# A four-layer graph network: half of a gather and two sets of transposes placed behind their product, and small f32 matmuls turned into rounded ones with two-part operands

## The chip, the core and the metric

The kernel runs on one core of one Trainium2 chip. The metric is the device time of one execution in microseconds (us). An execution that was profiled has a span, from its first to its last instruction, and its own device time, which is a little more.

The engines have short names in the rows: PE is the matmul engine (TensorE), PEld its weight loads, DVE is VectorE, ACT is ScalarE, POOL is GpSimd, and SP (SyncE) issues most of the DMAs.

## The reference

Four layers work on x, of shape 8 x 2048 x 64 (batch, nodes, features), with one 2048 x 2048 adjacency whose rows are normalised. Each layer is followed by a residual sum and a layer norm. Only what the change touches is shown.

```python
# layer 0: graph convolution with Chebyshev terms and weights made from node embeddings
As = [eye(N), A, 2 * A @ A - eye(N)]
x_g = einsum('knm,bmc->bnkc', stack(As), x)
out = einsum('bnki,nkio->bno', x_g, einsum('nd,dkio->nkio', embedding, weight)) + embedding @ bias

# layer 1: 64 hyperedges; H says which nodes belong to which edge
h = x @ W
s = leaky_relu(h @ a_node, 0.2)
alpha = softmax(where(H.T > 0, s, NEG))            # over an edge's nodes
agg = einsum('ben,bnf->bef', alpha, h)
beta = sigmoid((h @ a_gn)[:, None, :] + (agg @ a_ge)[:, :, None])
all_he = elu(beta * h + (1 - beta) * agg)          # per node and edge
coefs1 = softmax(where(H > 0, se, NEG))            # over a node's edges
g = einsum('bne,benf->bnf', coefs1, all_he)
```

Layers 2 and 3 are further products with the adjacency.

## The kernel before, in words

**Tiles and two-part operands.** The nodes are 16 tiles of 128. A tile of x is 128 rows of 512 columns (8 batches of 64 features). The adjacency is used as a 0/1 mask times a scale for each row. An operand of a large product is kept as two rounded parts, a high and a low one (`x_hi` and `x_lo`, `y_hi` and `y_lo`), that are multiplied by the mask one after the other. `r_(...)` marks an operand as rounded f32; such a matmul is one instruction on PE, and one whose operands are not marked is two.

**Order.** Inside `program_order()` the instructions of PE, DVE, ACT and POOL keep the order in which the code issues them. SP isn't bound in this way: its order is chosen by the planner that places the DMAs. Where a queue waits, all that stands behind it on that engine waits too.

**The first product** (`first_product`, matmuls at L569) makes y = A x for all tiles. It goes through 32 pieces of the adjacency, in four quarters of 8, with 512 target columns a quarter. A piece has two row tiles, and after the 8 matmuls of each row tile the loop may resume a generator of other work, `memberships`: once after the first row tile and twice after the second, from piece 9 on, and once in piece 6. At the end of each quarter ACT and DVE turn the sums into `y_hi` (L583) and `y_lo` (L584).

**The lists** (`memberships`) say for layer 1 which edges a node belongs to. Every `yield` ends a step. For each of four quarters q of the nodes: DVE makes `pT` (L382); PE counts with a triangular matrix into `pf` (L386); DVE makes `pfm` from it (L391, the tile is named `pT_raw`) and the first one-hot lists (L393, L396), whose stores and the next quarter's loads are issued there. Then come, for each of four tiles: `sm` on PE (L406) and `S` on DVE (L409, L412); `rk` on DVE (L419); a second matmul into `sm` (L424); its comparison on DVE (L429). `pf` and all `sm` share one PSUM buffer (tag `li`), so the next of them waits until DVE has read the one before.

**The end of the first product** transposes tile 0 of y (L594) for layer 0, then makes tile 0 of the second product, y2 = 2 A y (L603, scaled by ACT at L608).

**Layer 0** goes through the tiles j in order, each in eight groups of weight matmuls (`weigh`, PE L1446, DVE L1457). After the fifth group `visit(j)` does, on PE: the gather of tile j-2 into the edges' sums (L1651, a high and a low part), the first transposes of tile j+1 (`first_terms`), the second product of tile j+1 (`product`, L1403, 32 matmuls), in `counted` the degree (L1426) and the share of tile j-2 in the softmax denominators (L1430), the features' transposes `trx` of tile j-1, and the transposes `try2` of y2 of tile j+1 (`second_term`). ACT scales y2 (L1409) and then copies the denominators (L1432) and the degree (L1434). `weighted` makes what a later gather reads: the members' matrix `md`, and exp(score) times h in two parts (POOL L1638 and L1644, ACT L1643). PSUM buffers of tag `tr` are two, in turn.

**Layer 1** is performed by a list of tokens. For each tile, `sx` reads the terms of a node's at most three separate edges (L864), those of the shared slots (L868: `S` against `hgr`), and a transpose of `S`; `gates` on DVE (L884 to L889) forms gates and coefficients from them. `reciprocals` fills half of `hgr` (L808 to L810).

Lines are those of the kernel before.

Of the kernel before, what the change touches and what calls it, by code (L numbers as in the profile page):

```python
# [63 lines left out]
def kernel(  # L64
# [252 lines left out]
    def memberships(pre, ps, pm, fcw_sb, fcb_sb, fcg_sb):  # L317
# [60 lines left out]
        for q in range(NQ):  # L378
# [7 lines left out]
            nc.tensor.matmul(  # L386
                pf, r_(tri.rearrange("p h e -> p (h e)")), r_(pT), start=True, stop=True
            )
            yield
            pfm = raw  # L390
            nc.vector.tensor_tensor(pfm, pf, pT, ALU.mult)  # L391
            oh01 = pre.tile([P, QW], F32, tag="oh01", name=f"oh01_{q}", bufs=2)
# [60 lines left out]
    def first_product(own, pre, rawp, mskp, y_hi, y_lo, prepare, after, bias_in, midway, own_masks):  # L453

        x_hi, x_lo = buffer(own, 0, "x_hi"), buffer(own, 1, "x_lo")
        with tc.tile_pool(name="acc0", bufs=7, space=PSUM) as ps_acc, tc.tile_pool(
# [87 lines left out]
            with program_order():  # L544
# [43 lines left out]
                for _ in steps:  # L588
                    pass
                nc.vector.tensor_scalar(cols_of["s2"], cols_of["s1"], 2.0, None, op0=ALU.mult)  # L590
                tr = ps_acc.tile([P, NP, P], F32, tag="acc", name="try1_0")
                for pr in range(NP):
                    for part in (y_hi, y_lo):
# [6 lines left out]
                acc = ps_acc.tile([P, BC], F32, tag="acc", name="y2p_0")  # L600
                for mt in range(NT):
                    for part in (y_hi, y_lo):
                        nc.tensor.matmul(  # L603
                            acc, r_(own_masks[mt // 8][:, mt % 8, :]), r_(part[:, mt, :]),
                            start=mt == 0 and part is y_hi, stop=mt == NT - 1 and part is y_lo,
                        )
                y2 = own.tile([P, BC], F32, tag="b0_10", name="y2_0")
                nc.scalar.activation(y2, acc, AF.Copy, scale=cols_of["s2"][:, 0:1])  # L608
        return {"y1": y1T, "y2n": y2}

    @with_exitstack
    def layer1(
# [18 lines left out]
        mhalf = l1.tile([P, B], F32, tag="mhalf", name="mhalf")  # L631
        nc.gpsimd.memset(mhalf, -0.5)
        ext = l1.tile([P, 2, B], F32, tag="ext", name="ext")
        av32 = l1.tile([P, 32], F32, tag="av32", name="av32")
        nc.gpsimd.tensor_copy(av32, av_sb.to_broadcast([P, 32]))

# [70 lines left out]
        with tc.tile_pool(name="fa", bufs=2) as fa:  # L707
# [10 lines left out]
            with program_order():  # L718
# [135 lines left out]
        def units(j, dst):  # L854
# [4 lines left out]
            def sx():  # L859
                oh = l1.tile([P, 4, P], F32, tag="oh", name=f"oh_{j}", bufs=4)  # L860
                nc.sync.dma_start(oh, lists["oh"][j // 4][:, j % 4])
                sm = ps_s.tile([P, QW], F32, tag="sm", name=f"sx_{j}")
                for u in range(4):
                    nc.tensor.matmul(  # L864
                        sm[:, P + 16 * u:P + 16 * u + 16], r_(oh[:, u, :]), r_(extv),
                        start=True, stop=True,
                    )
                nc.tensor.matmul(  # L868
                    sm[:, P + 64:P + 80], S[:, j, :], hgr[:, j].rearrange("p k b -> p (k b)"),
                    start=True, stop=True,  # L870
                )
                transpose(sm[:, 0:P], S[:, j, :])
                t.update(oh=oh, sm=sm)
# [5 lines left out]
            def gates():  # L879
                gate = small("gate", f"gate_{j}", (P, 4, B))  # L880
                coef = small("coef", f"coef_{j}", (P, 4, B), 3)
                ex = t["sm"][:, P:P + 80].rearrange("p (u k b) -> p u k b", u=5, k=2)
# [385 lines left out]
    def layer0(  # L1268
# [6 lines left out]
        h_sb, wb, vecs, av_sb, pm, es, hgr, aggp, rden, early = layer1s  # L1275
        (raws, msk), terms, resid, norm, srow = begun, {}, {}, {}, {}
        x1s, xTs, hss, mds, scs, isplit, mms, tr15, dens = {}, {}, {}, {}, {}, {}, {}, [], {}

        homes = {"xT": (0, 1, 2), "xs": (3,), "ihi": (4,), "hs": (5,), "hsf": (15,), "y1T": (6, 7), "r": (8, 9),
                 "y2": (10,), "y2T": (11, 12), "cs": (13, 14)}  # L1280
# [141 lines left out]
        def counted(j, i):  # L1422

            dp = ps_tr.tile([P, QW], F32, tag="tr", name=f"dgp_{j}")
            if j < NT:
                nc.tensor.matmul(  # L1426
                    dp[:, 0:2], r_(msk[j, "sum"]), r_(ones_r), start=True, stop=True
                )
            if i >= 0:
                nc.tensor.matmul(dp[:, 8:8 + B], mds[i], es[:, i, :], start=True, stop=True)  # L1430
                dens[i] = tile("den", f"den_{i}", (P, B), 1)
                nc.scalar.copy(dens[i], dp[:, 8:8 + B])  # L1432
            if j < NT:
                nc.scalar.copy(deg[:, j:j + 1], dp[:, 0:1])  # L1434

# [193 lines left out]
        def weighted(j):  # L1629

            md = tile("md", f"md_{j}", (P, 2, E))
            nc.gpsimd.tensor_copy(r_(md), pm[:, j, :].unsqueeze(1).to_broadcast([P, 2, E]))
            mds[j] = md.rearrange("p h e -> p (h e)")
            if j < len(kept_i):
                for t, kept_part in zip(parts_of(j), kept_i[j]):
                    nc.sync.dma_start(kept_part, t)
            hs = tile("hsf", f"hs_{j}")
            nc.gpsimd.tensor_tensor(  # L1638
                b_view(hs), b_view(h_sb[:, j, :]), bcast(es[:, j, :]), ALU.mult
            )  # L1640
            hi = tile("hs", f"hs_hi_{j}")
            lo = tile("y1" if j == NT - 2 else "x1", f"hs_lo_{j}", bufs=1)
            nc.scalar.copy(r_(hi), hs)  # L1643
            nc.gpsimd.tensor_tensor(r_(lo), hs, hi, ALU.subtract)  # L1644
            hss[j] = hi, lo

        def gather(j):
            for part in hss[j]:
                if j == NT - 2 and part is hss[j][1]:
                    early[0](2)  # L1650
                nc.tensor.matmul(  # L1651
                    aggp, r_(mds[j]), r_(part), start=j == 0 and part is hss[0][0], stop=False
                )

        def spread():

# [43 lines left out]
        load_x(1)  # L1700
        def visit(j):

            when(j - 2, gather)
            if j < NT - 1:
                when(j - 1, normed, 1)
            when(j + 1, compare, 0)
            if j < NT - 1:
                when(j - 1, normed, 2)
            when(j + 1, first_terms)
            if j + 1 < NT:  # L1710
                for _ in product(j + 1):
                    pass
# [1 line left out]
            when(j + 2, mask, 1)  # L1714
            when(j + 1, compare, 1)
            counted(j + 1, j - 2)
            when(j - 1, to_features)
            if j == NT - 2:
                for t in range(len(kept_i)):
# [1 line left out]
                        nc.sync.dma_start(y[:, t, :], kept_part)  # L1721
            when(j + 1, second_term)
            if j == 2:
                nc.vector.tensor_copy(rden, dens[j - 2])
            elif j > 2:
                nc.vector.tensor_tensor(rden, rden, dens[j - 2], ALU.add)

        def last_tile():

            last = NT - 1  # L1730
            early[0](6)
            half_features(0)
            gather(last - 1)
# [969 lines left out]
```

## Time and profile before

| what | value |
|---|---|
| median of 3 runs | 1202.68 us (1201.78 to 1206.43) |
| the profiled execution | 1202.65 us |
| its span | 1200.9 us, 19838 instructions |
| granted TensorE clock | 0.998 |
| PE busy | 1179.7 us (98%) |
| DVE, POOL, ACT busy | 887.0 us (74%), 499.7 us (42%), 389.3 us (32%) |
| first product, 9 to 137 us | PE 125.32 busy of 128.00 |
| layer 0's visits, 171 to 620 us | PE 445.61 busy of 449.00, DVE 368.25 |
| layer 1, 664 to 936 us | PE 270.69 busy of 272.00, DVE 230.34 |

A row of the timeline gives the start and the duration in us, the engine, the line, the operation, what it writes and reads, and how many instructions were merged into it; in square brackets is how long the engine was idle before it and whom it waited for. The ends of matmuls are modelled and they overlap, so the distance between two starts says what a matmul costs. A row of the waits gives the waiting engine and line, whom it waited for, the total in us, how often, and the longest.

### The profile page before, as it was taken

The numbers are of one execution on the slowest core, as the hardware profiler recorded it, in microseconds if no ns is written. First come the engines' busy times: TensorE is split into PE (matmuls) and PEld (weight loads), VectorE is DVE, ScalarE is ACT, GpSimd is POOL, SyncE is SP. The second block draws the span as 40 slices with busy tenths as digits, with TensorE's granted clock in tenths as the row PEclk, the third lists the DMA queues.
The fourth block names the chain that finished last, engine by engine and source line by source line (L and its number), as shares of the span: only waits on it lengthen the run. The fifth ranks groups of instructions, "written<-read, shape, count | busy, mean of one in ns | idle before, by whom it ended". The sixth has DMA issues, their size and how long they took to land.

```text
span 1200.9 us, 19838 instructions
## 1 busy us (share of the span) xinstructions
PE 1179.7 (98%) x7502; PEld 942.4 (78%) x7502; DVE 887.0 (74%) x1677; ACT 389.3 (32%) x1005; POOL 499.7 (42%) x429
## 2 busy tenths in 40 slices
PE   9999999999999999999999999999999999999997
PEld 7877788888888888888887666666667888888886
DVE  4555668888888888888877788988887666665455
ACT  3100101222222222222223467767777321211111
POOL 2000392555545555555531489888871211100000
PEclk9999999999999999999999999999999999999999
DMA  8977852323332233333283313323220433434552
GB/s 287 250 226 226 180 166 94 113 91 117 117 112 94 94 108 117 117 117 115 80 298 137 111 71 114 99 77 106 97 71 1 148 133 106 140 106 168 183 175 73
DMA packets 101991, 157.10 MB, mean 131 GB/s; under 512 B 13056, under 2 KB 64640, under 8 KB 96256
## 3 DMA queue, kind: packets, MB, share of 16 engines
q1 hardware_dynamic: 97088, 151.51, 39.1%
q10 hardware_dynamic: 4368, 4.20, 1.0%
q8 instruction: 61, 1.00, 0.4%
q0 software_dynamic: 432, 0.05, 0.1%
q14 instruction: 42, 0.34, 0.1%
HBM read 117.97 MB, written 37.76 MB: 130 GB/s over the span
## 4 chain that ended last, share of the span: by engine, by line
PE 93%; DVE 2%; ACT 2%; DMA 1%; issue 1%; POOL 0%; SPq 0%; ACTq 0%; POOLq 0%; DVEq 0%
PE pp L1446 27%; PE a L1910 19%; PE ind L1910 10%; PE y2p L1403 9%; PE y1p L569 9%; PE fc L1028 3%; PE try L168 1%; PE yp L2009 1%; PE gp L929 1%; PE trm L168 1%; PE red L978 1%; PE u L1139 1%; PE hp L1571 1%; PE dp L947 1%; ACT y L1409 1%; PE aggp L1651 1%
## 5 line engine op out<-in xcount | busy, mean ns | idle before, releaser
L1457 DVE SCALAR_TENSOR_TENSOR r<-pp,emb_sb,r 128x256 f32<-128x256 f32 x512 | 247.6, 484 | 76.0 <-PE pp L1446 61.9
L1446 PE MATMUL pp<-w_sb,xT 64*128 64x256 f32 x1024 | 155.4, 380 | 0.6 <-DVE r L1457 0.6
L1446 PE MATMUL pp<-w_sb,y2T 64*128 64x256 f32 x1024 | 153.4, 376 | 0.0
L1446 PE MATMUL pp<-w_sb,y1T 64*128 64x256 f32 x1024 | 153.3, 376 | 0.0
L1315 POOL TENSOR_TENSOR ms<-msk,srow 128x1024 f32<-128x1024 f32 x30 | 76.2, 2540 | 89.9 <-DVE msk L449 89.9
L1446 PEld LDWEIGHTS pp<-w_sb,y2T 64*128 64x128 f32 x1024 | 99.3, 187 | 11.4 <-DVE y2T L1419 0.3
L1446 PEld LDWEIGHTS pp<-w_sb,y1T 64*128 64x128 f32 x1024 | 99.4, 187 | 11.2
L1446 PEld LDWEIGHTS pp<-w_sb,xT 64*128 64x128 f32 x1024 | 95.1, 187 | 12.9 <-issue 2.7
L569 PE MATMUL y1p<-x_hi,m 128*128 128x512 f32 x256 | 102.9, 402 | 0.7 <-ACT x_hi L471 0.7
L569 PE MATMUL y1p<-x_lo,m 128*128 128x512 f32 x256 | 100.5, 393 | 0.2 <-DVE x_lo L472 0.2
L1910 PE MATMUL a<-y_lo,mj_l 128*128 128x512 f32 x240 | 95.1, 396 | 0.0
L1910 PE MATMUL a<-y_hi,mj_l 128*128 128x512 f32 x240 | 95.0, 396 | 0.0
L1403 PE MATMUL y2p<-y_hi,msk 128*128 128x512 f32 x240 | 94.7, 395 | 0.0
L1910 PE MATMUL a<-v_hi,mj_l 128*128 128x512 f32 x240 | 93.9, 392 | 0.0
L1910 PE MATMUL a<-v_lo,mj_l 128*128 128x512 f32 x240 | 93.7, 391 | 0.0
L1403 PE MATMUL y2p<-y_lo,msk 128*128 128x512 f32 x240 | 93.6, 390 | 0.0
L1910 PE MATMUL ind<-y_hi,mj_l 128*128 128x512 f32 x208 | 90.5, 435 | 0.0
L1910 PE MATMUL ind<-y_lo,mj_l 128*128 128x512 f32 x208 | 81.8, 393 | 0.0
L964 POOL TENSOR_TENSOR ez<-ez,coef 128x1024 f32<-128x1024 f32 x32 | 61.6, 1926 | 11.1 <-DVE ez L959 11.0
L1355 DVE SCALAR_TENSOR_TENSOR ms<-ms,adj 128x1024 f32<-128x1024 f32 x30 | 66.2, 2206 | 0.0
L1638 POOL TENSOR_TENSOR hs<-h,es 128x512 f32<-128x512 f32 x15 | 15.7, 1043 | 115.8 <-ACT hgr L1610 115.8
L1111 POOL TENSOR_TENSOR r<-r,bias_sb 128x512 f32<-128x512 f32 x14 | 17.9, 1276 | 105.3 <-DVE r L2030 105.3
(347 smaller groups left out, 2460.5 us busy)
## 6 DMA issues: line engine op xcount, KB each, us to landing
mj_l<-mask SPq DMA_DIRECT2D x44, 1024.0 KB, 4.9
adj<-in_at SPq DMA_DIRECT2D x64, 256.0 KB, 3.8
mask<-msk SPq DMA_DIRECT2D x32, 512.0 KB, 4.5
raw<-in_at SPq DMA_DIRECT2D x31, 512.0 KB, 5.3
oh<-oh SPq DMA_DIRECT2D x32, 128.0 KB, 3.7
xT<-in_xt SPq DMA_DIRECT2D x16, 256.0 KB, 3.2
xs<-in_xn SPq DMA_DIRECT2D x16, 256.0 KB, 2.7
kept<-x SPq DMA_DIRECT2D x16, 256.0 KB, 3.6
```

The lines of the kernel that those rows point to most:

```text
L168: nc.tensor.matmul(dst, src, ident, start=True, stop=True, is_transpose=True)
L569: nc.tensor.matmul(accs[q][jj], r_(m[:, t, jj * P:(jj + 1) * P]), r_(part[:, mt, :]), start=i + h + t == 0 and part is x_hi, stop=i == 3 a ...
L964: nc.gpsimd.tensor_tensor(by_b(ezs[i]), by_b(ezs[i]), per_b(t["coef"], 2 * i, 2), ALU.mult)
L1028: nc.tensor.matmul(fcs[i][:, h, :], fcw_sb[rs], t["sT", i][rs], start=True, stop=True)
L1111: nc.gpsimd.tensor_tensor(b_view(t), b_view(t), bias2_sb.unsqueeze(1).to_broadcast([P, B, C]), ALU.add)
L1315: nc.gpsimd.tensor_tensor(ms, m, srow[j].unsqueeze(1).to_broadcast([P, 8, P]), ALU.mult)
L1355: nc.vector.scalar_tensor_tensor(ms, ms, 1.0, raws[j][h], op0=ALU.mult, op1=ALU.not_equal, accum_out=bad[:, 2 * j + h:2 * j + h + 1],)
L1403: nc.tensor.matmul(acc, r_(msk[j, mt // 8][:, mt % 8, :]), r_(part[:, mt, :]), start=mt == 0 and part is y_hi, stop=mt == NT - 1 and part ...
L1446: nc.tensor.matmul(pp[:, h, pl, :], terms[j][name][rs, 2 * bq + pl], w_sb[rs, k, dq * 4 * C:(dq + 1) * 4 * C], start=k == 0, stop=k == K - 1,)
L1457: nc.vector.scalar_tensor_tensor(rb, ppv[:, :, dd, :], emb_sb[:, j, d:d + 1], rb, op0=ALU.mult, op1=ALU.add)
L1638: nc.gpsimd.tensor_tensor(b_view(hs), b_view(h_sb[:, j, :]), bcast(es[:, j, :]), ALU.mult)
L1910: nc.tensor.matmul(acc, r_(a[:, mt, :]), r_(part[:, mt, :]), start=mt == 0 and part is hi, stop=mt == NT - 1 and part is lo,)
```

## The change

- In the first product, the transposes of tile 0 of y come behind the second product of tile 0 and ACT's scaling of it, instead of ahead of them.
- In a visit of layer 0, only the low part of the gather stands ahead of the product; in visits 2 to 14 the high part stands behind `counted`. In visit 0 the first transposes of tile 1 stand behind `counted` too.
- The denominators of tiles 0 to 13 are made from exp(score) in two rounded parts (`es2`, made by ACT and POOL in `weighted`), with one matmul of 16 columns; the 16 sums are added up in `dsum` and folded to 8 in the last visit.
- In layer 1, `hgr` is split into two rounded parts (`hgs`, two DVE operations in `reciprocals`, which runs twice), and the slots' terms are one rounded matmul of 32 columns, whose halves `gates` adds.
- In `memberships`, the `yield` between `pf` and `pfm` is gone.

```diff
@@ memberships
                 pf, r_(tri.rearrange("p h e -> p (h e)")), r_(pT), start=True, stop=True
             )
-            yield
             pfm = raw
             nc.vector.tensor_tensor(pfm, pf, pT, ALU.mult)
@@ first_product
                 nc.vector.tensor_scalar(cols_of["s2"], cols_of["s1"], 2.0, None, op0=ALU.mult)
+                (the product y2p_0 of 32 matmuls, and y2_0 = acc * s2 on ACT)
                 tr = ps_acc.tile([P, NP, P], F32, tag="acc", name="try1_0")
...
                 nc.scalar.copy(y1T, tr)
-                (the same product and y2_0)
@@ layer1
+        hgs = l1.tile([P, NT, 2, 2, B], F32, tag="hgs", name="hgs")
...
                     nc.vector.reciprocal(hgr[:, lo:hi, 1, :], rec)
+                    nc.vector.tensor_copy(r_(hgs[:, lo:hi, 0]), hgr[:, lo:hi])
+                    nc.vector.tensor_tensor(
+                        r_(hgs[:, lo:hi, 1]), hgr[:, lo:hi], hgs[:, lo:hi, 0], ALU.subtract
+                    )
...
-                    sm[:, P + 64:P + 80], S[:, j, :], hgr[:, j].rearrange("p k b -> p (k b)"),
+                    sm[:, P + 64:P + 96], r_(S[:, j, :]),
+                    r_(hgs[:, j].rearrange("p i k b -> p (i k b)")),
...
+                slot = small("slot", f"slot_{j}", (P, 2, B))
+                nc.vector.tensor_copy(slot, ex[:, 4])
+                nc.vector.tensor_tensor(slot, slot, ex[:, 5], ALU.add)
...
-                    nc.vector.tensor_copy(dst_[:, 3, :], ex[:, 4, k, :])
-                    nc.vector.tensor_tensor(dst_[:, 3, :], ex[:, 3, k, :], dst_[:, 3, :], op)
+                    nc.vector.tensor_tensor(dst_[:, 3, :], ex[:, 3, k, :], slot[:, k, :], op)
@@ layer0, counted
-                nc.tensor.matmul(dp[:, 8:8 + B], mds[i], es[:, i, :], start=True, stop=True)
-                dens[i] = tile("den", f"den_{i}", (P, B), 1)
-                nc.scalar.copy(dens[i], dp[:, 8:8 + B])
+                nc.tensor.matmul(
+                    dp[:, 8:8 + 2 * B], r_(mds[i]), r_(es2s[i].rearrange("p k b -> p (k b)")),
+                    start=True, stop=True,
+                )
+                dens[i] = tile("den", f"den_{i}", (P, 2 * B), 1)
+                nc.scalar.copy(dens[i], dp[:, 8:8 + 2 * B])
@@ layer0, weighted
+            if j < NT - 2:
+                es2s[j] = tile("es2", f"es2_{j}", (P, 2, B))
+                nc.scalar.copy(r_(es2s[j][:, 0, :]), es[:, j, :])
+                nc.gpsimd.tensor_tensor(
+                    r_(es2s[j][:, 1, :]), es[:, j, :], es2s[j][:, 0, :], ALU.subtract
+                )
@@ layer0, gather and visit
-        def gather(j):
-            for part in hss[j]:
-                if j == NT - 2 and part is hss[j][1]:
-                    early[0](2)
-                nc.tensor.matmul(
-                    aggp, r_(mds[j]), r_(part), start=j == 0 and part is hss[0][0], stop=False
-                )
+        def gather(j, i):
+            nc.tensor.matmul(
+                aggp, r_(mds[j]), r_(hss[j][i]), start=j == 0 and i == 1, stop=False
+            )
...
-            when(j - 2, gather)
+            for i in (1, 0) if j == NT - 1 else (1,):
+                when(j - 2, gather, i)
...
-            when(j + 1, first_terms)
+            if j:
+                when(j + 1, first_terms)
...
             counted(j + 1, j - 2)
+            if j == 0:
+                first_terms(1)
+            if 2 <= j < NT - 1:
+                gather(j - 2, 0)
             when(j - 1, to_features)
...
             if j == 2:
-                nc.vector.tensor_copy(rden, dens[j - 2])
+                sums.append(tile("dsum", "dsum", (P, 2 * B), 1))
+                nc.vector.tensor_copy(sums[0], dens[0])
             elif j > 2:
-                nc.vector.tensor_tensor(rden, rden, dens[j - 2], ALU.add)
+                nc.vector.tensor_tensor(sums[0], sums[0], dens[j - 2], ALU.add)
+            if j == NT - 1:
+                nc.vector.tensor_tensor(rden, sums[0][:, 0:B], sums[0][:, B:2 * B], ALU.add)
```

In the last tile the two parts of its gather are issued as before, with the same two steps of other work between them.

More of the change, by code (lines that the diff above doesn't have):

```diff
@@ L590, in first_product @@
                 nc.vector.tensor_scalar(cols_of["s2"], cols_of["s1"], 2.0, None, op0=ALU.mult)
+                acc = ps_acc.tile([P, BC], F32, tag="acc", name="y2p_0")
+                for mt in range(NT):
+                    for part in (y_hi, y_lo):
+                        nc.tensor.matmul(
+                            acc, r_(own_masks[mt // 8][:, mt % 8, :]), r_(part[:, mt, :]),
+                            start=mt == 0 and part is y_hi, stop=mt == NT - 1 and part is y_lo,
+                        )
+                y2 = own.tile([P, BC], F32, tag="b0_10", name="y2_0")
+                nc.scalar.activation(y2, acc, AF.Copy, scale=cols_of["s2"][:, 0:1])
                 tr = ps_acc.tile([P, NP, P], F32, tag="acc", name="try1_0")
@@ L599, in first_product @@
                 nc.scalar.copy(y1T, tr)
-                acc = ps_acc.tile([P, BC], F32, tag="acc", name="y2p_0")
-                for mt in range(NT):
-                    for part in (y_hi, y_lo):
-                        nc.tensor.matmul(
-                            acc, r_(own_masks[mt // 8][:, mt % 8, :]), r_(part[:, mt, :]),
-                            start=mt == 0 and part is y_hi, stop=mt == NT - 1 and part is y_lo,
-                        )
-                y2 = own.tile([P, BC], F32, tag="b0_10", name="y2_0")
-                nc.scalar.activation(y2, acc, AF.Copy, scale=cols_of["s2"][:, 0:1])
         return {"y1": y1T, "y2n": y2}
@@ L881, in gates @@
                 coef = small("coef", f"coef_{j}", (P, 4, B), 3)
-                ex = t["sm"][:, P:P + 80].rearrange("p (u k b) -> p u k b", u=5, k=2)
+                ex = t["sm"][:, P:P + 96].rearrange("p (u k b) -> p u k b", u=6, k=2)
+                slot = small("slot", f"slot_{j}", (P, 2, B))
+                nc.vector.tensor_copy(slot, ex[:, 4])
+                nc.vector.tensor_tensor(slot, slot, ex[:, 5], ALU.add)
                 for dst_, k, op in ((gate, 0, ALU.add), (coef, 1, ALU.mult)):
@@ L1277, in layer0 @@
         x1s, xTs, hss, mds, scs, isplit, mms, tr15, dens = {}, {}, {}, {}, {}, {}, {}, [], {}
+        es2s, sums = {}, []
         homes = {"xT": (0, 1, 2), "xs": (3,), "ihi": (4,), "hs": (5,), "hsf": (15,), "y1T": (6, 7), "r": (8, 9),
@@ L1645, in weighted @@
             hss[j] = hi, lo
-        def gather(j):
-            for part in hss[j]:
-                if j == NT - 2 and part is hss[j][1]:
-                    early[0](2)
-                nc.tensor.matmul(
-                    aggp, r_(mds[j]), r_(part), start=j == 0 and part is hss[0][0], stop=False
-                )
+        def gather(j, i):
+            nc.tensor.matmul(
+                aggp, r_(mds[j]), r_(hss[j][i]), start=j == 0 and i == 1, stop=False
+            )
         def spread():
@@ L1732, in last_tile @@
             half_features(0)
-            gather(last - 1)
+            gather(last - 1, 0)
+            early[0](2)
+            gather(last - 1, 1)
             denp = ps_p.tile([P, 2, 2, 4 * C], F32, tag="pp", name="denp")[:, 0, 0, 0:B]
```

## The prediction

> **What bounds the kernel now.** I read the page's first part and its chain first, then who TensorE (PE) waits for, then the timeline at the places that the diff touches.
>
> ```profile
> PE 1179.7 (98%) x7502; PEld 942.4 (78%) x7502; DVE 887.0 (74%) x1677; ACT 389.3 (32%) x1005; POOL 499.7 (42%) x429
> PE 93%; DVE 2%; ACT 2%; DMA 1%; issue 1%; POOL 0%; SPq 0%; ACTq 0%; POOLq 0%; DVEq 0%
> ```
>
> PE is busy for 98% of the span and makes 93% of the chain: what lengthens or shortens PE's own sequence counts in full, anything else only where PE waits for it. These are all of PE's waits that the diff can touch:
>
> ```profile
> PE try L168 <- ACT deg L1434: 4.2, 15, 0.8
> PE sm L406 <- DVE oh L429: 1.2, 3, 0.4
> PE sm L406 <- DVE pT_raw L391: 1.1, 1, 1.1
> PE try L168 <- ACT y L608: 0.8, 1, 0.8
> PE sm L424 <- DVE rk L419: 0.4, 1, 0.4
> ```
>
> The first and fourth follow a product in layer 0, and the diff moves matmuls into them. The other three lie in the first product, where the list steps are dealt out between its matmuls, and the diff takes one `yield` from these steps. A gap as it stands on PE (first product, third quarter):
>
> ```profile
> 98.98 0.40 PE L569 MATMUL y1p<-x_lo,m 128*128 128x512 f32 x1
> 99.22 0.22 PE L424 MATMUL sm<-S,rk 128*128 128x128 f32 x1
> 99.83 0.30 PE L406 MATMUL sm<-tri,pT 128*128 128x64 f32 x1 [0.39 <-DVE oh L429]
> 99.96 0.48 PE L569 MATMUL y1p<-x_hi,m 128*128 128x512 f32 x1
> 100.28 0.39 PE L569 MATMUL y1p<-x_lo,m 128*128 128x512 f32 x1
> ```
>
> Starts count here, since durations overlap; plain matmuls start 0.23 us apart. L424 and the next tile's L406 stand next to each other, and between them VectorE (DVE) must read the one PSUM buffer of tag `li` (L429). A visit of layer 0:
>
> ```profile
> 358.23 0.39 PE L1403 MATMUL y2p<-y_lo,msk 128*128 128x512 f32 x1
> 358.46 0.17 PE L1426 MATMUL dgp<-ones_r,both 128*128 128x2 f32 x1
> 358.48 0.37 PE L1430 MATMUL dgp<-es,md 128*128 128x8 f32 x2
> 358.71 0.64 PE L168 MATMUL trx<-ident,x 128*128 128x128 f32 x4
> 359.57 0.66 PE L168 MATMUL try<-ident,y 128*128 128x128 f32 x4 [0.23 <-ACT deg L1434]
> ```
>
> After the product, ScalarE (ACT) copies y2, den and deg (358.72 to 359.52), and only then may `try2` start, 1.34 us after the product's last matmul, however little PE has in between.
>
> **The change part by part.** *The removed `yield`.* The steps are resumed once after the first row tile of a piece and twice in a row after the second, from piece 9 on; eight product matmuls lie between the resumptions except inside the pair. Call resumption number c, c=0 being the lone one in piece 6: c mod 3 = 1 is the single one, 2 and 0 are the pair. Four segments precede quarter 0, and a quarter has 16 (pT, pf, pfm with the one-hots, then for each of four tiles sm, rk, L424 with the next segment beginning with L429). So `pf` falls on 2, 0, 1, 2 in the four quarters. The trace shows this: the L406 after pf comes 8, 16, 8, 8 product matmuls later, and only the third quarter has L424 and L406 as neighbours. Without the `yield` a quarter has 15 segments, a multiple of three: all four have `pf` on 2 and their first L406 on 0. Then every quarter has the third's order, and pf and the first L406 become neighbours too.
>
> Price of a neighbour pair L424/L406: from 98.98 to 100.28 are 1.30; two plain intervals are 0.46, and the two steps set apart cost 0.11 and 0.12 (58.65 to 59.22, 60.61 to 61.19). Lost: 0.61. Price of pf/L406: pf to DVE's L391 is 0.43 (93.34 to 93.77), L391 lasts 0.69, L406 starts 0.04 later (75.66 to 75.70): 1.16, with 0.23 ahead and 0.13 and 0.32 behind 1.84, less 0.46 and less 0.36 that they cost apart (0.24 and 0.12): 1.02. Queued behind the waiting L391 on DVE are the one-hots, S and the next piece's mask. The masks are about 9 us ahead (piece 16's done at 62.3, needed at 70.8), so PE doesn't run out of them. The step also issues four one-hot stores and two loads of the next quarter's lists on SP, whose queue then stands until DVE has the one-hots; behind them are the pieces' loads. The same lead covers that; uncovered, it is the kind of wait that DVE's masks had for loads (L527, 6.0 us in 5 waits), and I leave it at nothing.
>
> Before, by the same subtraction: second quarter 1.37 (74.20 to 76.15, L391 behind y_lo), third 0.61+0.61+1.26 (the last with y_lo ahead of rk), fourth 0.24: 4.1 us. After: 4 x 1.02 = 4.1, 12 x 0.61 = 7.3, again 0.65 where y_lo falls in the third quarter, and 1.4 in the second, where y_lo now stands between the first L406 and its L424 (DVE needs 1.4 for one-hots and S, 2.7 for y_lo, 0.7 for a mask, 0.5 for rk = 5.3, against 16 matmuls and L406's own, 3.9). Sum 13.5. **Net +9.4**; from +7 (if y_lo is covered) to +12 (if DVE is late at a third of the pairs by what y_lo cost).
>
> *Tile 0's transposes behind its product* (L594): eight at 0.11, 136.93 to 137.77 = 0.84, go into the gap 144.90 to 146.11 while ACT makes y2. But the third y2T matmul group already waits 0.30 for DVE's y2T (147.67), which is behind compares and a mask that wait for loads. PE moves later against these loads by the waits above, so this cover partly lifts: between 0 and -1.1, I take **-0.7**. y1T's copy (0.60) now follows y2's on ACT and has the four transposes and the first xT group (1.1 us) to hide under; without that, 0.3 are lost.
>
> *Tile 1's transposes* (L1390, 160.42 to 161.36): into the idle 0.78 before `try2` (169.62) of visit 0, which stays bound by ACT: **-0.9** (0 to -0.94).
>
> *Half of the gather* (L1651): the high half starts 0.34, the low 0.24 ahead of its successor, and the first after f32 work pays 0.10 for the switch, which the low half will now pay. So 0.235 each leave the front of the product in visits 2 to 14. Behind it: `dgp` 0.02, the denominator 0.11, the gather 0.235, `trx` about 0.47, in all 0.84 plus 0.23 from the last product matmul = 1.07 < 1.34. 13 x 0.235 = **-3.06**; nothing is gained if ACT's chain were longer by as much (see below), so 0 to -3.4. What waits behind the moved matmul is `trx`, whose copy on ACT stands behind deg anyway.
>
> *Denominators as two parts*: one rounded matmul for two f32 ones (358.48 to 358.71); hidden in the visits, **-0.1** in visit 15. The den copy grows from 8 to 16 columns: 0.155 as against 0.17 for deg's one column, so no size shows; nothing. es2 adds an ACT copy and a POOL subtraction 14 times, each bounded by 0.3 (POOL's 128x128 md copy); POOL waits 0.73 there for hs_hi (L1644, 11.0 in 15), and the gather comes a visit later. Uncovered they would cost up to 0.3 x 14 = 4.
>
> *Slots' terms* (L868): two f32 matmuls starting 0.11 apart (672.20, 672.31, 672.42) become one with 32 columns. L864's rounded ones with 16 also start 0.11 apart. 16 x 0.11 = **-1.8** (-0.9 if 32 columns add half; -2). DVE keeps six operations in gates. Splitting hgr adds two DVE operations twice, 0.2 to 0.35 each by the rows around (L808, L726); DVE idles 1.90 before L808 and 0.56 before L884. If the second pair sticks out, 0.1.
>
> [...]
>
> Sum: +9.4 - 0.7 - 0.9 - 3.06 - 0.1 - 1.8 = +2.8. The profiled execution took 1202.65 (span 1200.9 and 1.75 around it), the median is 1202.68, so one sum serves both: **1205.5**.
>
> **The rivals.** (1) *DVE late, slower.* At the pairs DVE isn't waiting for PE but still at a mask, as with y_lo in the third quarter (1.26 for 0.61). For: that row. Against: DVE idled 2.59 and 2.36 before the other two L429. If it holds for ten pairs, 10 x 0.65 = +6.5: 1212. It decides from the point where DVE's work per three segments exceeds PE's 16 matmuls, 3.7 us; the rows (S 0.6, mask 0.7, rk 0.5, L429 0.3) give 2.1. (2) *The re-phasing costs nothing*, since the removed step changes only DVE's place and PE's four lost segments are made up: then only the gains stay, -6.6: 1196.1. Against: the third quarter is the same order, and it lost. (3) *The moves bring nothing*: ACT's chain after the product grows by what PE saves. Then +9.4 - 0.1 - 1.8 = +7.5: 1210. Against: den and deg are ready for copying before y2 is.
>
> **How the numbers follow.** Forecast 0.65, with its own range 1202 to 1209; (1) 0.17, 1208 to 1213; (2) 0.08; (3) 0.10, 1207 to 1210.5. About 0.5% (6.0 us: 1196.7 and 1208.7) is what a measurement can tell. Slower by more: 0.12 of (1), 0.05 of (3), 0.01 of the forecast: 0.18. Faster by more: 0.06 of (2). Same: 0.76. The range 1199.5 to 1210.5 leaves out (2) and half of (1).
>
> **What would show it.** In the changed profile: PE's L406 waiting for L429 about 12 times for some 5 us, and for L391 4 times; the first product ending some 9 us later; `try2` still 1.34 us after each product, with less idle before it; L868 as 16 matmuls. Wrong would be: few L406 waits (then (2)), or no shorter visit than 31.8 us.

## The result and the profile after

| what | before | after |
|---|---|---|
| median of 6 runs each, side by side | 1203.63 us (1201.78 to 1206.43) | 1209.1 us (1207.75 to 1211.35) |
| ratio, 95% interval | | 1.0047 (1.003 to 1.0064) |
| the profiled execution | 1202.65 us | 1211.29 us |
| its span, and granted clock | 1200.9 us, 0.998 | 1208.6 us, 0.994 |

The changed kernel is slower by 0.47%. That is 3.6 us above the forecast of 1205.5, inside the range of 1199.5 to 1210.5, and within the half per cent called the same. It lies just above the range that the forecast itself was given (1202 to 1209) and inside those of the rivals (1) and (3). So the time alone does not tell whose account is right; the profile and the experiments have to.

From here on, lines in the profiles after are those of the changed kernel: the product `y1p` is L568, `sm` is L405 and L423, the one-hots L428, `pfm` L390, tile 0's transposes L602 and their copy L607. The page after, its first part and its chain:

```profile
PE 1184.2 (98%) x7472; PEld 943.7 (78%) x7472; DVE 882.9 (73%) x1682; ACT 391.9 (32%) x1019; POOL 499.8 (41%) x443
PE 91%; DVE 4%; ACT 2%; issue 1%; POOL 1%; DMA 0%; SPq 0%; ACTq 0%; DVEq 0%; POOLq 0%
```

There are 30 matmuls fewer and 14 operations more on each of ACT and POOL. PE is 4.5 us busier with less work (the half-clock stretch below is a part of it), and 2% of the chain have passed from PE to DVE. Whom PE waits for says where:

```profile
PE sm L405 <- DVE oh L428: 4.7, 12, 0.5
PE sm L405 <- DVE pT_raw L390: 3.1, 4, 0.8
PE sm L423 <- DVE rk L418: 0.8, 2, 0.4
PE try L168 <- ACT y1T L607: 0.7, 1, 0.7
PE try L168 <- ACT deg L1445: 0.4, 1, 0.4
```

The first two are the neighbours that the removed step created: 12 and 4, as many as were counted out. The last was 4.2 us in 15 waits and is 0.4 in one: the moved matmuls lie in the wait for ACT. The fourth is new and was not foreseen.

The same marks on PE in both traces (start of the operation named, in us; profiled executions). The `dgp` of tile 0 comes ahead of the visits, and that of tile j+1 stands in visit j:

| mark | before | after | difference | change in this stretch |
|---|---|---|---|---|
| last matmul of the first product | 136.70 | 145.33 | +8.63 | +8.63 |
| first group of layer 0 (`pp`) | 146.70 | 155.08 | +8.38 | -0.25 |
| `dgp` of tile 0 | 154.84 | 163.10 | +8.26 | -0.12 |
| `dgp` of tile 1, visit 0 | 168.68 | 176.07 | +7.38 | -0.88 |
| `dgp` of tile 2, visit 1 | 198.91 | 206.33 | +7.42 | +0.04 |
| `dgp` of tile 15, visit 14 | 613.00 | 617.22 | +4.22 | -3.20 in visits 2 to 14 |
| end of layer 0 (`trhe`) | 661.02 | 665.11 | +4.09 | -0.13 |
| last `sx` of layer 1 | 870.59 | 877.79 | +7.20 | +3.11 |
| end of layer 1 | 905.00 | 912.57 | +7.57 | +0.37 |
| end of the span | 1200.94 | 1208.59 | +7.65 | +0.08 |
| the execution's time | 1202.65 | 1211.29 | +8.64 | +0.99 |

Two rows hold something for which the prediction has no term. The first is layer 1: there the profiled execution after has a stretch in which PE was granted half its clock, and that of before has none. Two windows that begin about 10 us behind the first `trhe`, first after, then before (the columns are the window, its length, the busy time and instructions of PE, PEld, DVE, ACT and POOL, the granted clock, the DMA share and GB/s):

```profile
675.00:685.00 10.00, 10.00 (x28) 7.69 (x29) 6.21 (x20) 2.05 (x10) 4.76 (x3) 0.50 0.00 0
```

```profile
671.00:681.00 10.00, 9.59 (x48) 7.14 (x48) 7.68 (x20) 5.68 (x20) 4.76 (x3) 1.00 0.09 27
```

28 matmuls instead of 48 in 10 us, at 0.50. It costs some 3.9 us of the 8.64 (the 3.48 of the layer and the 0.41 that the slots' part gains alone), and it is not the change's doing: of 78 runs of the kernel before, 27 had a mean clock at or below 0.995, with medians some 3.9 us above the rest (1207.19 to 1203.31, 1206.87 to 1203.06 and 1206.61 to 1202.63 in three sets). So medians with few runs carry how often it fell, and below, where that matters, runs without it are compared. Without it the changed kernel takes 1208.5 (4 of the 6 runs).

The other row is the last: 1.0 us more between the end of the span and the end of the execution.

### The profile page after: what moved, and what is told of

Its sections match the earlier page's. It is cut to its first block, busy times and chain, and to the rows that moved or that the text cites. A ratio compares the mean times of both kernels' runs of the same rounds, so it can differ in the third digit from the quotient of the medians.

```text
span 1208.6 us, 19826 instructions
## 1 busy us (share of the span) xinstructions
PE 1184.2 (98%) x7472; PEld 943.7 (78%) x7472; DVE 882.9 (73%) x1682; ACT 391.9 (32%) x1019; POOL 499.8 (41%) x443
## 4 chain that ended last, share of the span: by engine, by line
PE 91%; DVE 4%; ACT 2%; issue 1%; POOL 1%; DMA 0%; SPq 0%; ACTq 0%; DVEq 0%; POOLq 0%
PE pp L1457 27%; PE a L1935 19%; PE y1p L568 9%; PE y2p L1411 9%; PE ind L1935 9%; PE fc L1035 3%; PE try L168 1%; PE yp L2034 1%; PE gp L936 1%; PE u L1146 1%; PE trm L168 1%; PE hp L1582 1%; PE dp L954 1%; PE red L985 1%; ACT y L1417 1%
## 5 line engine op out<-in xcount | busy, mean ns | idle before, releaser
L568 PE MATMUL y1p<-x_hi,m 128*128 128x512 f32 x256 | 102.3, 399 | 0.4 <-DVE y_lo L583 0.3
L568 PE MATMUL y1p<-x_lo,m 128*128 128x512 f32 x256 | 100.1, 391 | 0.2 <-DVE x_lo L471 0.2
L971 POOL TENSOR_TENSOR ez<-ez,coef 128x1024 f32<-128x1024 f32 x32 | 61.6, 1925 | 11.0 <-DVE ez L966 10.9
```

Source lines behind the costliest of these rows:

```text
L568: nc.tensor.matmul(accs[q][jj], r_(m[:, t, jj * P:(jj + 1) * P]), r_(part[:, mt, :]), start=i + h + t == 0 and part is x_hi, stop=i == 3 a ...
L971: nc.gpsimd.tensor_tensor(by_b(ezs[i]), by_b(ezs[i]), per_b(t["coef"], 2 * i, 2), ALU.mult)
```

## The experiments

Each was timed beside the kernel before on the same chip.

**Putting the `yield` back into the changed kernel.**

```diff
                 pf, r_(tri.rearrange("p h e -> p (h e)")), r_(pT), start=True, stop=True
             )
+            yield
             pfm = raw
```

> The changed kernel with the one yield put back between pf and pfm. Theory A (the neighbour steps on PE cost the first product its +8.6): the first product ends at 136 to 137 us as before, PE waits there at L405/L406 4 times and not 16, the moves and the rounded sums keep what they gained (4.4 us by the start of layer 1), and the time is 1197 to 1200 us. Theory B (the first product is late for another reason, the new order at its end or the loads): it still ends 5 us or more late, time 1205 to 1209. The half-clock stretch of 10 us that the changed kernel's profile has at the start of layer 1 is not explained by either; if it belongs to the moved or rounded work it stays here.

Measured: 1200.13 us (1198.53 to 1202.33) beside 1204.32, ratio 0.9966 (0.9953 to 0.9979). That is just above the 1197 to 1200 expected. The first product ends at 135.93, 0.8 ahead of before instead of 8.6 behind, and 0.6 of the 0.8 lies ahead of its first matmul. PE waits at `sm` L406 four times, and not 16. `trhe` stands at -4.77; behind the first product 4.0 are gained, where the changed kernel gains 4.5. From its first matmul to its last the first product takes 8.9 us less than in the changed kernel, and the medians differ by 9.0 (by 8.4 without the runs at a clock of 0.995 or less).

**Removing only the `yield` from the kernel before.**

```diff
-            yield
             pfm = raw
```

> The kernel before with that one yield removed and nothing else. Theory A: PE's waits on L428/L429 and L390/L391 appear as in the changed kernel (12 and 4 times), the first product ends 8 to 9.5 us later, time 1211 to 1213 us. Theory B: within 3 us of before.

Measured: 1211.19 us (1211.02 to 1215.26), ratio 1.0058 (1.0039 to 1.0078). PE's waits for the one-hots (4.7 in 12) and for `pfm` (3.1 in 4) are those of after to the digit, the first product ends 8.59 late, and all visits of layer 0 keep just that (+8.52 in visit 0, +8.49 in visit 14). The medians differ by 6.9, since more of the runs beside it were at a clock of 0.995 or less (9 of 24, against 1 of 5); among runs at a clock of 0.998 or more it is 1211.1 (4 runs) beside 1202.5 (10 runs), 8.6 as in the marks. Nothing is made up later: the rival in which the re-phasing costs nothing is out.

**Shifting the steps by two, and by one.** If the cost lies in which resumption a step falls on, then empty steps ahead of the quarters must move it without touching any work. 15 steps a quarter are a multiple of three, so one shift holds for all quarters.

```diff
+        for _ in range(2):
+            yield
         for q in range(NQ):
```

> The changed kernel, yield still gone, with two empty steps ahead of the quarter loop of the lists, so that every quarter's pf falls on the single resumption and no second sum matmul has the next tile's first beside it. Theory A (which steps are neighbours on PE sets the cost, not how many steps there are): the first product loses nearly nothing, ends 3 to 4 us earlier than before's (133 to 134 us), time 1193 to 1196 us. Rival (15 steps a quarter are slow whatever their place, since DVE and the stores come too early): first product late by 5 us or more, time about 1208.

Measured: 1196.6 us (1195.9 to 1200.54) beside 1204.32, ratio 0.9948 (0.9929 to 0.9967). The time is just above the 1193 to 1196 expected. The first product ends at 132.83, 3.87 ahead of before; from its first matmul to its last it takes 3.5 less, and the rest lies ahead of its first matmul. Of the three rows of `sm` in PE's waits one is left, and the place in the third quarter where neighbours stood reads on the timeline as in the second fence:

```profile
PE sm L407 <- DVE oh L430: 0.2, 1, 0.2
```

```profile
93.40 0.39 PE L570 MATMUL y1p<-x_lo,m 128*128 128x512 f32 x1
93.63 0.19 PE L407 MATMUL sm<-tri,pT 128*128 128x64 f32 x1
93.65 0.48 PE L570 MATMUL y1p<-x_hi,m 128*128 128x512 f32 x1
...
95.36 0.39 PE L570 MATMUL y1p<-x_lo,m 128*128 128x512 f32 x1
95.59 0.22 PE L425 MATMUL sm<-S,rk 128*128 128x128 f32 x1
95.65 0.45 PE L570 MATMUL y1p<-x_hi,m 128*128 128x512 f32 x1
```

L407 and L425 stand alone, 1.96 us apart, and neither has a bracket: PE waits for DVE at neither. In the changed kernel the pair stands together, with 0.61 between its starts and the bracket that names the one-hots:

```profile
101.51 0.40 PE L568 MATMUL y1p<-x_lo,m 128*128 128x512 f32 x1
101.75 0.22 PE L423 MATMUL sm<-S,rk 128*128 128x128 f32 x1
102.36 0.30 PE L405 MATMUL sm<-tri,pT 128*128 128x64 f32 x1 [0.39 <-DVE oh L428]
102.49 0.48 PE L568 MATMUL y1p<-x_hi,m 128*128 128x512 f32 x1
102.81 0.39 PE L568 MATMUL y1p<-x_lo,m 128*128 128x512 f32 x1
```

101.51 to 102.81 is 1.30, the price that the prediction had read from such a place before.

One empty step instead of two:

> As the one before, with one empty step instead of two: pf stands on the second of the pair. Theory A by the same count: no neighbours of L423 and L405, but in the second quarter L423 comes 4.0 us after pf while DVE needs 6.3 (y_lo is between), and in the third L428 is behind y_lo: losses of 2.3 and 1.6 us, so the first product ends about as before (136 to 138 us), time 1197 to 1200 us. Rival: the same as with none or two empty steps, about 1208 us.

Measured: 1199.83 us (1198.81 to 1203.72), ratio 0.9968 (0.995 to 0.9986); the first product ends at 135.57. The many waits are gone here too, but three single ones remain: 1.1 for the one-hots, 0.9 for `rk` and 0.9 for `y_lo`. It was expected to end at 136 to 138, with dearer waits (2.3 and 1.6). So removing the `yield` is neither good nor bad: from the first matmul to the last of the first product, the same 15 steps cost 8.7 us, win 0.7 or win 3.5 by where the first of them falls.

**The moves alone.** The kernel before with the moved transposes and the moved half of the gather.

```diff
-            when(j - 2, gather)
+            for i in (1, 0) if j == NT - 1 else (1,):
+                when(j - 2, gather, i)
...
             counted(j + 1, j - 2)
+            if j == 0:
+                first_terms(1)
+            if 2 <= j < NT - 1:
+                gather(j - 2, 0)
```

> The kernel before with only the moves: tile 0's and tile 1's first transposes and the high half of the gather behind the product; no two-part sums. Theory: visit 0 gains 0.9, visits 2 to 14 gain 0.23 each (3.0), the end of the first product 0.25; 4.1 us by the start of layer 1. With two f32 matmuls for the denominators there is 0.11 more ahead of the moved gather, which the 1.34 us of ACT's chain still cover, so the gain a visit is the same as in the whole change. Rival (the moved gather needs the shorter denominators to fit): gains under 0.15 a visit. Time 1200 to 1201.

Measured: 1198.61 us (1197.5 to 1204.17) beside 1203.5, ratio 0.9962 (0.9947 to 0.9977). The tail gains 0.25, visit 0 0.88, visits 2 to 14 0.25 each; `trhe` stands at -4.87, of which -0.51 was already there when the first product ended. The time is below the 1200 to 1201 expected, in part for that. The rival in which the moves bring nothing is out.

**The slots' terms alone.** The kernel before with `hgs`, the rounded matmul of 32 columns and `slot`.

```diff
-                    sm[:, P + 64:P + 80], S[:, j, :], hgr[:, j].rearrange("p k b -> p (k b)"),
+                    sm[:, P + 64:P + 96], r_(S[:, j, :]),
+                    r_(hgs[:, j].rearrange("p i k b -> p (i k b)")),
```

> The kernel before with only layer 1's part: hgr split in two rounded parts and the slots' terms as one rounded matmul of 32 columns. Theory C (PE saves its 16 x 0.11 here, but the tiles then wait for DVE and give most of it back): the start of layer 1 stands as before, the last slots' matmul is 0.8 to 1.3 us earlier than before's relative to it, the stage's end (first matmul of layer 2's features) only 0.3 to 0.7; time 1203 to 1204. Rival (the rounded matmul saves in full and the given-back time belongs to the moves in layer 0): stage end 1.5 us or more earlier. The kernels with the whole change have 1.0 us more outside their span than before (2.75 against 1.75); if that belongs to this part it shows here.

Measured: 1203.45 us (1201.78 to 1206.91) beside 1203.5, ratio 0.9995 (0.9977 to 1.0013). From the end of layer 0 to the last `sx` PE is 0.81 ahead, at layer 1's end 0.41. Mark by mark each `sx` gains its 0.11, as priced, and other marks in between fall back by about 0.1 at a time: at `gp` and `red`, and at the transposes of g, whose wait for DVE in PE's waits was 0.2 in one before and is here:

```profile
PE trm L168 <- DVE g L989: 0.6, 2, 0.4
```

So PE's gain of 1.76 in matmuls is still there in the work and mostly gone in the time. The largest step back is the last, 0.35 at the transposes of g of the last tile. There DVE is what ends last, and PE arriving earlier only waits longer. The layer starts 0.54 late here, since a wait of 1.0 for `y2T` came in at the start of layer 0. The edit has no part in that place, and the wait needs no edit: the two profiled executions of the two empty steps, one and the same program, have none and 0.8 (below).

**The denominators alone.** The kernel before with `es2`, the one matmul of 16 columns, and `dsum`.

```diff
-                nc.tensor.matmul(dp[:, 8:8 + B], mds[i], es[:, i, :], start=True, stop=True)
+                nc.tensor.matmul(
+                    dp[:, 8:8 + 2 * B], r_(mds[i]), r_(es2s[i].rearrange("p k b -> p (k b)")),
+                    start=True, stop=True,
+                )
```

> The kernel before with only the denominators of layer 0 as two-part sums (es2, one rounded matmul of 16 columns, dsum). By the prediction's step the saved matmul is covered by ACT's chain in every visit: the visits keep their length within 0.03 us, 0.1 us is saved in visit 15, time within 1 us of before. Rival (the ACT copy and the POOL subtraction cost, or the shorter row of matmuls counts): visits longer or shorter by 0.1 us or more, 1.4 us in all.

Measured: 1203.59 us (1202.32 to 1208.77), ratio 0.9995 (0.9981 to 1.001). The visits keep their length (+0.39 in visit 0, +0.28 in visit 14), visit 15 gains 0.10. But from the last matmul to the end of the execution it is 10.9 us, against 10.1 before; here the longer end lies inside the span, with 1.57 outside it.

**Tile 0's transposes in a PSUM buffer of their own**, on top of the two empty steps, since the wait for `y1T` was the one new wait:

```diff
-                tr = ps_acc.tile([P, NP, P], F32, tag="acc", name="try1_0")
+                tr = ps_s.tile([P, NP, P], F32, tag="li", name="try1_0")
```

> As the one with two empty steps, and tile 0's first transposes go into the PSUM buffer of the lists (tag li) instead of the pool of the sums, whose place the transposes of layer 0 take over. Theory D (the end of the first product gained 0.25 and not 0.84 because try2 of tile 0 waits for the copy of y1T that frees this pool): try2's wait on y1T (0.7 us) is gone, it waits for y2 alone, and layer 0's first weight matmul is 0.5 us earlier against the end of the first product; 0.4 to 0.6 us less time, 1195.5 to 1196.3. Rival (DVE's chain of compares and masks ends last): the weight matmuls of y2T wait for DVE instead and nothing is gained.

Measured: 1200.74 us (1195.0 to 1203.89), ratio 0.9974 (0.9957 to 0.999); 7 of its 12 runs were at a clock of 0.995 or less. The wait for `y1T` is gone and the first group of layer 0 comes earlier against the end of the first product, but only until its third part. Its row in PE's waits, and the timeline there:

```profile
PE pp L1459 <- DVE y2T L1429: 1.0, 1, 1.0
```

```profile
141.20 0.27 PE L604 MATMUL try<-ident_r,y_lo 128*128 128x128 f32 x1
...
141.47 0.66 PE L168 MATMUL try<-ident,y 128*128 128x128 f32 x4
...
143.58 0.68 DVE L1429 TENSOR_TENSOR y2T<-try,xT 128x512 f32<-128x512 f32 x1
...
144.32 0.49 PE L1459 MATMUL pp<-w_sb,y2T 64*128 64x256 f32 x2 [1.03 <-DVE y2T L1429]
```

`try2` starts without a bracket, 0.27 after the last transpose. DVE's `y2T` comes 2.1 us later, behind a mask operation of 1.75, and PE waits 1.03 there. Not all of the 1.03 is owed to the buffer, since DVE's chain is itself late by a varying amount. The two empty steps alone, in their first and in their second profiled execution (the same program):

```profile
136.44 1.56 DVE L450 TENSOR_SCALAR msk<-adj 128x1024 fp32r<-128x1024 f32 x1 [0.89 <-DMA adj<-in_at]
...
142.99 0.68 DVE L1429 TENSOR_TENSOR y2T<-try,xT 128x512 f32<-128x512 f32 x1
...
143.72 0.70 PE L1459 MATMUL pp<-w_sb,y2T 64*128 64x256 f32 x4
```

```profile
137.12 1.54 DVE L450 TENSOR_SCALAR msk<-adj 128x1024 fp32r<-128x1024 f32 x1 [1.80 <-DMA adj<-in_at]
...
143.64 0.68 DVE L1429 TENSOR_TENSOR y2T<-try,xT 128x512 f32<-128x512 f32 x1
...
144.37 0.70 PE L1459 MATMUL pp<-w_sb,y2T 64*128 64x256 f32 x4 [0.77 <-DVE y2T L1429]
```

The mask waits for a load that came 0.7 later in the second. But in the first too, PE's third part starts 0.05 after `y2T` has ended (143.67): with DVE as early as there, removing the wait for `y1T` would gain nothing. The spans do not contradict that: among runs at a clock of 0.998 or more they are 1192.2 and 1193.4 here, against 1193.2 to 1194.0 with the two empty steps alone and 1192.8 to 1195.8 in their repetition. That cannot tell half a microsecond.

**The microsecond at the end, and the parts that pay.** Every version so far with the denominators in two parts had it. The next two leave them as before, on top of the two empty steps; the third is the two empty steps again, beside them.

> The changed kernel with two empty steps ahead of the quarter loop, and with the denominators as before (no exp(score) in two parts, no dsum). Theory A, the denominators part costs about 1 us behind the last instruction's store and gives nothing in the visits: 1195.6 in an execution without a half-clock stretch, span 1193.9, 1.7 outside the span instead of 2.6 to 2.9; visits 1 to 14 as with the part (each 0.24 shorter than before); visit 15 longer by 0.1. Theory B, the microsecond at the end has another cause that the part only went along with: 2.6 to 2.9 outside the span stay, 1196.6.

> The kernel before with the moved transposes and the moved half of the gather, with the yield between pf and pfm removed and two empty steps ahead of the quarter loop; neither the denominators nor the slots' terms in two parts. Theory A (denominators cost 1 us at the end, slots give 0.4 by the end of layer 1): 1196.0, span 1194.3, 1.7 outside the span. Theory B (the end has another cause): 1197 with 2.6 to 2.9 outside the span. In both, the first product ends about 3.9 earlier than before (near 132.8) and layer 1's last sx stands 0.8 later than with the slots' terms in two parts, relative to its first.

> The changed kernel with two empty steps ahead of the quarter loop once more, beside the two others on the same chip: 1196.6, span 1193.6 without a half-clock stretch, 2.6 to 2.9 outside the span.

Measured, beside 1204.55 of the kernel before:

| kernel | median of all runs | ratio, 95% interval | runs at a clock over 0.995 | outside the span |
|---|---|---|---|---|
| no denominators | 1199.2 (1195.31 to 1200.67) | 0.9944 (0.9925 to 0.9964) | 1195.48 (3 of 8) | 1.67 to 1.74 |
| moves only | 1196.36 (1194.32 to 1200.13) | 0.9933 (0.9911 to 0.9956) | 1196.15 (5 of 6) | 1.67 to 1.75 |
| all parts, again | 1197.83 (1195.52 to 1201.47) | 0.9948 (0.9933 to 0.9964) | 1197.53 (9 of 12) | 2.72 to 2.97 |

The microsecond goes with the denominators and with no other part: six programs have the part and the longer end, and six (the one before among them) have neither. What in it makes the end longer stays open: the last instructions are the same and last as long, and only the time behind the last store's issue differs. The expectation for the version without the denominators (1195.6, 1.7 outside) was met in two of its runs (1195.31 and 1195.48, at 0.998 and 0.997); five of the other six were at 0.995 or less and one at 0.996, which is why its median is high. The moves with the two empty steps, without either of the two-part forms, are the fastest by the median: 0.67% faster than the kernel before, with intervals of the three that overlap.

## Why the prediction was right or wrong

**Removed `yield`: +9.4 predicted, +8.63 measured (+8.59 alone).** Mechanism, counts and prices held: 12 and 4 waits, 1.30 for a place of L423 and L405, and for `pf` and L405 (96.45 to 98.32) 1.87 where 1.84 was summed up. Against the version with two empty steps, whose steps stand alone, the first product is 12.2 longer after (13.5 in the sum) and 3.5 longer before (4.1). The part that was too dear is `y_lo` in the second quarter. It was put at 1.4 in the wait for `rk`; that matmul lost 0.7 and a product matmul ahead of it 0.5. The rest of the 0.8 is spread over terms too small to tell apart.

**Tile 0's transposes: -0.7 predicted, -0.25 measured.** The step that failed is "y1T's copy (0.60) now follows y2's on ACT and has the four transposes and the first xT group (1.1 us) to hide under". The timeline after, end of the first product:

```profile
153.06 0.69 ACT L598 ACTIVATE y<-y2p,s 128x512 f32<-128x512 f32 x1 [6.24 <-PE y2p L593]
...
153.54 0.27 PE L602 MATMUL try<-ident_r,y_lo 128*128 128x128 f32 x1
...
153.85 0.58 ACT L607 COPY y1T<-try 128x512 f32<-128x512 f32 x1
...
154.49 0.66 PE L168 MATMUL try<-ident,y 128*128 128x128 f32 x4 [0.68 <-ACT y1T L607]
```

The transposes' PSUM tile comes from the pool of the sums (`ps_acc`), whose place layer 0's own transposes take over. So `try2` may not start before ACT has copied `y1T`, and that copy now stands behind y2's. 0.84 were taken from ahead of the product, 0.6 came back as this wait. I had followed the data and not the buffer. The run with another buffer, read beside the two empty steps alone, shows that this was worth less than it looked: the next wait, for DVE's `y2T`, is the cover that the prediction had named. The 0.30 that the prediction read there is the wait of the weight load; the matmuls behind it start 0.06 later than their usual 0.43. In the changed kernel `y2T` is in time, and up to the `dgp` of tile 0 the gain is 0.37.

**Tile 1's transposes: -0.9 predicted, -0.88 measured. Half of the gather: -3.06 predicted, -3.20 measured after, 13 times 0.25 alone.** The visit of the kernel after that answers to the one shown before, PE's rows of the timeline:

```profile
364.68 0.17 PE L1434 MATMUL dgp<-ones_r,both 128*128 128x2 f32 x1
364.71 0.26 PE L1438 MATMUL dgp<-es,md 128*128 128x16 f32 x1
364.82 0.48 PE L1665 MATMUL aggp<-hs_hi,md 128*128 128x512 f32 x1
365.13 0.60 PE L168 MATMUL trx<-ident,x 128*128 128x128 f32 x4
365.81 0.66 PE L168 MATMUL try<-ident,y 128*128 128x128 f32 x4
```

From `dgp` to `try2` it is 1.13, and 1.11 before: ACT's chain still sets the distance (its copy of the degree ends at 365.76), and the gather lies within it. The bracket that stood at `try2` is gone only because the modelled end of `trx` comes at 365.73. By the starts, the last matmul of `trx` stands 0.34 ahead of `try2` (0.51 before), where transposes start 0.11 apart. So about 0.23 of room are left, the size of one more such matmul; the moves alone, with 0.11 more in it, keep the distance.

**Denominators: -0.1 predicted.** In visit 15 it is -0.13 (-0.10 alone), and the uncovered bound of 4 us for `es2` did not come: the visits keep their length. But 1.0 us came at the end of the execution, in a place where the prediction had no term at all.

**Slots' terms: -1.8 predicted, -0.41 measured.** The price of a matmul was right (0.11 each). What failed was multiplying it by 16 as if PE alone set the pace of layer 1: three quarters are given back between the tiles. Even PE's share of this stage (270.69 of 272.00) hid that, since the durations of matmuls are modelled and overlap. At the transposes of g, the brackets name DVE for about 0.45 of the 1.35 given back, and single ones elsewhere DVE, ACT or POOL; who ends the rest is not shown.

**The sum.** By the marks, with the half-clock stretch left out: up to the end of layer 0 the prediction had +4.64 and the trace has +4.09. Then -0.4 instead of -1.8, and +1.0 at the end: +4.7, against the +5.5 of the medians. The three misses in size, 0.45, 1.4 and 1.0, all lie on the side of a slower kernel, and the re-phasing's 0.8 on the other. That it offsets part of them is luck.

**The rivals.** DVE late at the pairs: PE's longest wait for the one-hots is 0.5, and the pair measured as priced, so DVE was not behind a mask there. Nor was a lower clock behind the waits a part of the loss: in the kernel before, the matmuls behind the wait of 1.5 us (74.20 to 75.70) start 0.23 apart again and the granted clock from 66 to 78 is 1.00, and with all 16 waits it is 1.00 in each of four windows from 30 to 145 us.

## What to carry to other kernels

When steps of other work are dealt out by a counter, count on which resumption each step falls before and after an edit: here one `yield` less moved every producer next to its consumer, and two empty steps turned a loss of 8.7 us in the first product into a gain of 3.5. A step that is moved takes its buffer along, so ask who gets the place next and what now stands ahead of its reader (here the 0.84 taken from ahead of the product brought a wait of 0.68 for `y1T`). A saving on the busiest engine need not count in full: in layer 1, 1.76 us less on PE were worth 0.41, with waits of 0.6 for DVE at the transposes of g. Multiply one out only after looking at who ends last between two of its occurrences.

## What was not expected of the hardware

- Near the start of layer 1 PE's granted clock was 0.50 for 10.24 us in the profiled execution after. Five profiled executions show such a stretch in windows of 2 us: the changed kernel, the removed `yield` alone, the two empty steps in both of their profiles, and the two empty steps without the denominators. It lasts 10.2 in each, and begins 9.8 us after layer 1's first transposes in the changed kernel and 9.7 in the one without the denominators. One such stretch takes 0.004 off the mean clock of a span of 1201 us, and the runs of one program differ by that much: 27 of 78 of the kernel before have a mean of 0.995 or less, with medians some 3.9 us above those of the rest. Ahead of the stretch lies a head with sparse matmuls (PE 4.17 us busy in 6.00 after), in which no single wait of PE is over 0.9. The same head reads 4.19 in 6.00 in the profiled execution before, where the clock stays at 1.00. So what trips it stays open. The clock records of the trace after have 669.01 us at full clock, then the 10.24 at half, then 518.83 at full: 65.33 and 50.67 times 10.24, and the full stretch of the trace before, 1191.25, is 116.33 times it. In these two traces, then, all are multiples of a third of it.
- Two programs with the same last instructions can differ by 1.0 us behind the last of them: 1.66 to 1.83 us outside the span without the denominators in two parts, 2.57 to 3.04 with them and the other parts, and 1.44 to 1.61 with them alone, where the longer end lies inside the span. The cause is open.
- The wait for `y2T` at the start of layer 0 (up to 1.0) came and went in versions whose edit was elsewhere, and in two executions of one program (none and 0.8): the load for which DVE's mask waits there landed 0.7 later in the second.
